# Unread bfloat16 products in TensorE's gaps, and projections that do not wait for their bias

## The chip, the cores and the metric

One core of a Trainium2 chip runs the whole program. The metric is the device time of one execution in microseconds. The engines are TensorE (PE, its weight loads PEld), VectorE (DVE), ScalarE (ACT), GpSimd (POOL) and SyncE (SP), which issues most transfers; ScalarE issues some too.

## The reference

A decoder layer over 32 sequences of 128 tokens with 128 features: causal self-attention (16 heads of 8), cross-attention to `ctx_1024`, and a mixture of 8 experts of which each token takes 2. Each of the three is followed by a sum with its input and a layer norm.

```python
x = _layernorm(x + _attn(x, x, x, sa_wq, sa_bq, ..., True), ln1_g, ln1_b)
x = _layernorm(x + _attn(x, encoder_output, encoder_output, ca_wq, ca_bq, ..., False), ln2_g, ln2_b)
x = _layernorm(x + _moe(x, router_w, router_b, e_w1, e_b1, e_w2, e_b2), ln3_g, ln3_b)
```

In `_attn`, `Q = q_in @ wq + bq` and `K = k_in @ wk + bk`; the scores are the softmax's argument. In `_moe`, the two experts with the largest router weights get `gelu(x w1 + b1) w2 + b2`. All is float32.

## The kernel before

The sequences are worked on in 8 groups of 4. For each group and each attention there is a chain: load `xin`, four transposes on TensorE into a PSUM bank, a copy to `xT` (ScalarE), the projections, then scores.

A projection of queries or keys is made by `parts`. One float32 product of 128x512 (`project`, line 841 in the profile) goes to a bank. ScalarE adds the bias column and rounds to bfloat16 (`p3[:, 0]`, line 916), VectorE takes the rest (`u`, line 920), GpSimd splits that into two further bfloat16 parts (lines 924 and 927; for the first group's queries it is VectorE). Then transfers (`qk<-p`, line 949) spread the parts over the rows of `qk`, so that one bfloat16 product of 64 rows yields a float32-like score. Scores are made twice: with queries on the partitions, for the maxima (VectorE, `nm`, line 1045), and with keys on the partitions, for the exponentials (ScalarE, `pr`, line 1513). The maxima are split, transposed (line 1066), copied (`nmT`) and sent by a transfer (`qk<-nmT`, line 1078) into spare rows of the queries; the second scores wait for that. After the last attention step come the experts' blocks (lines 1859 and 1876).

The order of work is not the order of the code. Each piece is a `Task` with an engine, a planned duration, a priority, what it depends on (`deps`) and the buffers it holds (`Buf`, whose places come from pools; `s_ps` is the PSUM pool `Banks`, four tiles `ps` of two halves). `Plan.run` simulates the engines with the planned durations: a free engine takes the ready task of lowest priority whose buffers can be had. The result, `plan.order`, is a list by planned start, and `Plan.emit` writes the instructions in that list's order. On the chip each engine then works through its own instructions strictly in that order, and waits on semaphores where data is not there. Planned times only set the order. `early` adds a task outside the attention chain, such as a memset; `t1` in `parts` is the product, `t2` ScalarE's part, and the last entry of the `deps` that `parts` is given is the load (or the computation) of the bias column.

Of the kernel before, what the change touches and what calls it, by code (L numbers as in the profile page):

```python
# [9 lines left out]
F32 = mybir.dt.float32  # L10
BF16 = mybir.dt.bfloat16
I32 = mybir.dt.int32
U32 = mybir.dt.uint32
AF = mybir.ActivationFunctionType
# [3 lines left out]
P = 128  # L18
# [17 lines left out]


AHEAD = 4.0
LINK = 0.07
LEAD = 0.4  # L40
SWITCH = 0.06
# [157 lines left out]
class Plan:  # L199
# [21 lines left out]
    def run(self):  # L221
# [17 lines left out]
        while left:  # L239
# [68 lines left out]
            if what is not None:  # L308
                t, kind = what
                if kind == "end":  # L310
# [4 lines left out]
                    for s in t.next:  # L315
                        s.n -= 1
                        if s.n == 0:
# [3 lines left out]
                            else:  # L321
                                k += 1
                                late = LEAD if s.lead and t.lead and t.lat < 1.0 else 0.0
                                heapq.heappush(events, (now + LINK + late, k, (s, "ready")))
                elif kind == "apart":
# [7 lines left out]
        self.order = order  # L333
        return max(t.end for _, _, t in order)

    def emit(self, tc):
        sync = mybir.DependencyInfo(mybir.DependencyClass.Sync, mybir.DependencyReason.DATA)
        seen = {}

        def line(i):  # L340
            return (i.engine, "DMA" in i.opcode)

        for _, _, t in self.order:
            bb = tc.nc.cur_bb.bb
            if t.rest:
                self.pause()
            n0 = len(bb.instructions)
            t.fn()
            t.ins = list(bb.instructions[n0:])
            if not t.own:  # L350
                continue
            need = dict.fromkeys(t.deps)
            for b in t.bufs:
                need.update(dict.fromkeys(b.before))
            kept = [i for u in need for i in u.ins]
            mine = t.ins[0]
            for u in need:
                for i in u.ins if any(line(j)[1] for j in u.ins) else u.ins[-1:]:
                    if line(i) != line(mine) or line(i)[1]:
                        tc.add_manual_dep(mine, i.name, sync, reason="data or place")  # L360
            for i in t.ins:
                for key, name in seen.items():
                    if key[0] != i.engine or (key[1] and line(i)[1] and t.eng == "POOL"):
                        tc.declare_no_dep(i, group=name, keep=kept, reason="apart, by the plan")
            for i in t.ins:
                name = seen.setdefault(line(i), f"{i.engine}{'q' if line(i)[1] else ''}")
                tc.add_to_no_dep_group(name, i)
# [3 lines left out]
def kernel(  # L371
# [34 lines left out]
    nc = tc.nc  # L406
# [12 lines left out]
    plan = Plan()  # L419
    add = plan.add  # L420

    def sb(shape, name, dtype=F32):
        return one.tile(shape, dtype, name=name)
# [5 lines left out]
    s_ps = Banks([psum.tile([P, 2, 512], F32, name=f"ps{i}") for i in range(4)], 2)  # L429
# [23 lines left out]
    def early(eng, dur, prio, fn, deps=()):  # L453
        return add(eng, dur, prio, fn, deps)
# [6 lines left out]
    def c_ident():  # L461
# [3 lines left out]
            fill=1.0, base=0, channel_multiplier=1,  # L465
        )

    t_ident = early("POOL", 0.7, -20, c_ident)
    t_ident16 = early("DVE", 0.3, -19.9, lambda: nc.vector.tensor_copy(ident16, ident), [t_ident])

# [157 lines left out]
    def pe(dur, prio, fn, deps, bufs, mode="128x128", lat=0.0):  # L628
        return add("PE", dur, prio, fn, deps, bufs, mode=mode, lat=lat)

    b_q = Buf(s_ps)
    t = pe(
        0.3, -4, lambda b=b_q: nc.tensor.matmul(b.at[:, 0:1], lhsT=wqcr, rhs=cols["b1"], start=True, stop=True),
        [t_wqcr, t_col["b1"]], [b_q],
    )
# [5 lines left out]
    for n, wo in (("s", "wos"), ("c", "woc")):  # L641
        bv = Buf(s_ps)
        t = pe(
            0.3, -9 if n == "s" else 3,
            lambda bv=bv, n=n, wo=wo: nc.tensor.matmul(
                bv.at[:, 0:P], lhsT=cols["bv" + n].broadcast_to([P, P]), rhs=raw[wo], start=True, stop=True
            ),
            [t_col["bv" + n], t_raw[wo]], [bv],
        )
# [14 lines left out]
    def c_rwg():  # L664
# [5 lines left out]
    t = pe(  # L670
        0.3, 3.6,
        lambda br=br: nc.tensor.matmul(
            br.at[:, 0:E], lhsT=cols["b2"].broadcast_to([P, P]), rhs=rw, start=True, stop=True
        ),
        [t_rw, t_col["b2"]], [br],
    )
# [13 lines left out]
    t = pe(0.2, 12, lambda bb=bb: nc.tensor.transpose(bb.at[:, 0 : E * NFC], b1r, ident[: E * NFC, : E * NFC]), [t_b1r, t_ident], [bb], "32x128")  # L690
# [128 lines left out]
    first = {}  # L819
# [19 lines left out]
    def project(bank, w, xT):  # L839

        nc.tensor.matmul(bank, lhsT=w, rhs=xT.rearrange("p s t -> p (s t)"), start=True, stop=True)  # L841
# [67 lines left out]
    def parts(w, b, xT, deps, prio, terms, name):  # L909


        bank, p3, r1, at = Buf(s_ps), Buf(s_p3), Buf(s_r1), Buf(s_q if name[0] == "q" else s_kk)
        t1 = pe(1.12, prio, lambda: project(bank.at, w, xT.at), deps, [bank, xT, p3])
        t2 = add(
            "ACT", act(512, 1), prio + 0.1,
            lambda: nc.scalar.activation(p3.at[:, 0, :], bank.at, AF.Identity, bias=b), [t1], [bank, p3],
        )
        t3 = add(
            "DVE", dve(512), prio + 0.2,
            lambda: nc.vector.scalar_tensor_tensor(r1.at, bank.at, b, p3.at[:, 0, :], ALU.add, ALU.subtract),  # L920
            [t2], [bank, p3, r1],
        )
        eng, ename, du = (nc.vector, "DVE", (0.32, 0.69)) if name == "qs0" else (nc.gpsimd, "POOL", (0.62, 1.16))
        t4 = add(ename, du[0], prio + -3.68, lambda: eng.tensor_copy(p3.at[:, 1, :], r1.at), [t3], [p3, r1])  # L924
        t5 = add(
            ename, du[1], prio + -2.28,
            lambda: eng.tensor_tensor(p3.at[:, 2, :], r1.at, p3.at[:, 1, :], ALU.subtract), [t4], [p3, r1],  # L927
        )
        soon = name in ("qs0", "ks0")
        again = name[0] == "q" and name not in ("qs0", "qs1")  # L930
        q, dq = ("ACT", nc.scalar) if name == "ks0" else ("SP", nc.sync)
        n = 1 if name[1:] == "s0" else 2 if name[1:] == "s1" else 3
        cleared = t_qz[0:n] if name[0] == "q" else t_qz[3 : 3 + n]
        t7 = []
        if again:
            t7.append(
                add(
                    q, 0.6, prio + 0.4,
                    lambda: dq.dma_start(out=at.at[3::4].rearrange("a i n -> a (i n)"), in_=zero_d), [t4, t_zero, *cleared],
                    [at], lat=3.0,  # L940
                )
            )
        for k, t_ in enumerate((t2, t4, t5)):
            for t in range(8):
                if terms[t] != k + 1:
                    continue

                def rows(t=t, k=k):
                    dq.dma_start(out=at.at[t::8], in_=p3.at[:, k, :])  # L949

                t7.append(
                    add(q, 0.6, (-23 + 0.1 * k if soon else prio + 0.37) + 0.01 * t, rows, [t_, *cleared], [p3, at], lat=2.6)
                )
                if soon:
                    it_store.setdefault(name, []).append(t7[-1])
        return at, t7, t5
# [510 lines left out]
    at = {}  # L1467
# [5 lines left out]
    for i in range(NT + NL):  # L1473
# [18 lines left out]
        for h in range(2):  # L1492
            if sk is not None:
                w = sk[2]
# [4 lines left out]
                else:  # L1499
                    nd = [itk.nmt["s", sk[1], "lo"], itk.nmt["s", sk[1], w]]  # L1500
                kp, tk = Buf(s_ps, 2), Buf(s_tk)
                t = pe(
                    time_k(sk), i + 0.5 * h - AHEAD, lambda sk=sk, h=h, kp=kp: scores_k(sk, h, kp.at),
                    [t_cols, *itk.t_Q, *itk.t_K, *nd], [kp, itk.Q, itk.K, itk.pr[w], tk],
                    "64x64" if sk[0] == "s" else "64x128",
                )
# [4 lines left out]
                te = add(  # L1511
                    "ACT", 1.02, i + 0.5 * h + 0.1 - AHEAD,
                    lambda kp=kp, prb=prb, h=h: nc.scalar.activation(  # L1513
# [8 lines left out]
            if sq is not None:  # L1522
                itq = items[sq[0], sq[1]]
                qp, tq = Buf(s_ps, 2), Buf(s_tq)
                t = pe(
                    time_q(sq), i + 0.5 * h + 0.49 - AHEAD, lambda sq=sq, h=h, qp=qp: scores_q(sq, h, qp.at),
                    [t_cols, *itq.t_Q, *itq.t_K, steps_k.get(i - LOCK)], [qp, itq.Q, itq.K, nm, tq],
                    "64x64" if sq[0] == "s" else "64x128",
                )
                step_tasks[i] = t  # L1530
                scores_all.append(t)
                ms.append(maximum(sq, h, qp, nm, i + 0.5 * h + 0.93 - AHEAD, t, tq))
        if sq is not None:
# [187 lines left out]
    def load_numbers(name, engine, tab, s, n):  # L1721
# [13 lines left out]
    t = pe(  # L1735
        0.12, X0 - 1.9,
        lambda: nc.tensor.matmul(bf.at[:, 0:E], lhsT=ones16, rhs=cg[:, NG - 1, :], start=True, stop=True),
        [cg_done[NG - 1]], [bf],
    )
# [13 lines left out]
    for e in range(E):  # L1753

        def fill(e=e):
            own = rows_d[P + e * REG : P + (e + 1) * REG, :]
            nc.sync.dma_start(out=own[bass.ds(t_places["all"][e], P), :], in_=fillrow)
# [212 lines left out]
    at = 0  # L1970
# [4 lines left out]
    s = 0  # L1975
    for gi in range(NG):
        done = 2 * G * (gi + 1) + E - 1
        s = max((done if gi >= GF else NF + max(E, done - NF)) - 1, s + 4 if gi else 0)
# [3 lines left out]
    idle = sb([P, 176], "idle")  # L1982
    plan.pause = lambda: nc.gpsimd.memset(idle, 0.0)
    plan.run()
    plan.emit(tc)


# [39 lines left out]
```

## Time and profile before

| | |
|---|---|
| median of 3 runs | 554.89 us (554.87 to 559.47) |
| profiled execution | 559.5 us, span 557.8 us |
| mean granted TensorE clock | 0.903 |
| PE busy | 449.5 us, 81% of the span |
| VectorE, ScalarE, GpSimd busy | 66%, 54%, 57% |
| share of the chain that ended last | PE 45%, DVE 17%, DMA 15%, POOL 7% |

The span goes from the first to the last instruction of one profiled execution, and the time of that execution is 1.7 us longer. The granted clock is a share of full speed. The chain that ended last is followed back from the last instruction, at each step to what released it. A product of two float32 tiles appears as two records.

### The profile page before, as it was taken

To read this page: it belongs to the slowest core of one execution; us is meant where nothing else is said; L and a number is where in the kernel's file an instruction comes from. 1 tells how busy PE (TensorE), PEld (TensorE's weight loads), DVE (VectorE), ACT (ScalarE), POOL (GpSimd) and SP (SyncE) were. 2 spreads that over 40 slices of the span, in tenths; PEclk is the share of its full clock that TensorE was granted. 3 is DMA by queue.
4 is the path that set the end of the run, shared out by engine and by line. 5 is a ranking of instruction groups with operands and counts; after the bars stand their busy time and mean duration, and the time that the engine had idled before them with its cause. 6 is when DMAs were issued, how large, how long until landed. Compare 5 with 4: busy or idle time off the path is not lost.

```text
span 557.8 us, 22749 instructions
## 1 busy us (share of the span) xinstructions
PE 449.5 (81%) x8571; PEld 355.3 (64%) x8571; DVE 368.3 (66%) x1063; ACT 303.1 (54%) x684; POOL 320.3 (57%) x589
## 2 busy tenths in 40 slices
PE   6648687788878979869798888758999989999930
PEld 3424564565555557557566566537899989999930
DVE  6477465587849748659566858884747412288887
ACT  3324345367355564645646745527676657778840
POOL 3742423433425774774773764834488888767771
PEclk9767898889979978898898989977999989999975
DMA  5776633756536466376353251267872988896432
GB/s 165 129 166 163 142 84 77 174 138 184 161 90 165 116 156 166 84 194 175 92 145 89 79 158 27 71 173 231 233 236 88 343 262 258 264 301 201 120 92 89
DMA packets 104748, 87.59 MB, mean 157 GB/s; under 512 B 24235, under 2 KB 91983, under 8 KB 104160
## 3 DMA queue, kind: packets, MB, share of 16 engines
q1 hardware_dynamic: 98736, 76.69, 50.6%
q0 software_dynamic: 4320, 8.47, 4.5%
q8 instruction: 69, 1.13, 0.9%
q10 hardware_dynamic: 1584, 0.98, 0.7%
q14 instruction: 39, 0.32, 0.2%
HBM read 43.23 MB, written 13.97 MB: 103 GB/s over the span
## 4 chain that ended last, share of the span: by engine, by line
PE 45%; DVE 17%; DMA 15%; POOL 7%; issue 6%; SPq 5%; ACT 3%; POOLq 0%; ACTq 0%; DVEq 0%
PE ps L985 12%; PE ps L1859 10%; PE ps L1876 10%; DMA qk<-p 8%; DVE nm L1045 6%; DMA qk<-nmT 3%; SPq L949 3%; PE ps L841 3%; ACT pr L1513 2%; PE ps L877 2%; POOL rows_d L1399 2%; POOL p L927 2%; PE ps L835 1%; PE ps L1290 1%; PE ps L1826 1%
## 5 line engine op out<-in xcount | busy, mean ns | idle before, releaser
L1045 DVE TENSOR_REDUCE nm<-ps 128x8 f32<-128x1024 f32 (+1 forms) x112 | 132.8, 1217 | 47.4 <-PE ps L985 46.2
L1513 ACT ACTIVATE pr<-ps 128x1024 f32<-128x1024 f32 x112 | 110.8, 1021 | 56.4 <-PE ps L985 52.9
L985 PE MATMUL ps<-qk,qk 64*128 64x128 bf16 (+2 forms) x3072 | 95.3, 226 | 39.8 <-DMA qk<-p 12.7
L985 PEld LDWEIGHTS <-qk 64*64 64x64 bf16 (+1 forms) x3072 | 65.5, 112 | 83.4 <-issue 31.4
L1399 POOL DMA_INDIRECT rows_d<-y,rid x64 | 64.9, 1014 | 35.9 <-issue 12.9
L985 PE MATMUL ps<-pr,v 64*32 64x128 f32 (+2 forms) x3072 | 74.4, 272 | 8.6 <-issue 7.0
L985 PEld LDWEIGHTS ps<-pr,v 64*32 64x32 f32 (+1 forms) x3072 | 59.1, 113 | 21.6 <-issue 14.3
L1859 PE MATMUL ps<-qk,qk 128*128 128x128 f32 x488 | 63.9, 279 | 0.0
L1859 PEld LDWEIGHTS ps<-qk,qk 128*128 128x128 f32 x488 | 59.6, 195 | 0.4 <-issue 0.4
L1908 POOL DMA_INDIRECT res_d<-p,id x49 | 48.2, 984 | 15.6 <-DVE st L1181 5.4
L1868 ACT ACTIVATE qk<-ps,b1c 128x128 f32<-128x128 f32 x160 | 45.2, 387 | 17.1 <-PE ps L1859 14.9
L1058 POOL CAST nmx<-nm 128x16 bf16<-128x16 f32 x64 | 13.0, 203 | 69.5 <-DVE nm L1045 67.3
L1876 PE MATMUL ps<-wall,qk 128*128 x320 | 42.1, 278 | 0.3 <-ACT qk L1835 0.3
L1868 ACT ACTIVATE k<-ps,b1c 128x128 f32<-128x128 f32 x124 | 35.1, 382 | 12.5 <-PE ps L1859 10.9
L1876 PEld LDWEIGHTS ps<-wall,qk 128*128 128x128 f32 x320 | 38.9, 194 | 0.6 <-ACT qk L1835 0.4
L1141 DVE STREAM_TRANSPOSE u<-ps 128x512 f32<-128x512 f32 x32 | 22.1, 702 | 25.9 <-PE ps L985 17.4
L927 POOL TENSOR_TENSOR p<-u,p 128x512 bf16<-128x512 f32 x31 | 35.8, 1157 | 1.6
L924 POOL CAST p<-u 128x512 bf16<-128x512 f32 x31 | 19.1, 615 | 25.8 <-DVE u L920 16.6
L1876 PE MATMUL ps<-wall,k 128*128 x248 | 32.2, 275 | 0.0
L1876 PEld LDWEIGHTS ps<-wall,k 128*128 128x128 f32 x248 | 29.8, 192 | 0.0
L1908 POOL DMA_INDIRECT res_d<-o,id x22 | 22.0, 998 | 12.6 <-DVE rti L1350 5.7
L1889 DVE TENSOR_SCALAR id<-xT,tab_e 128x1 int32<-128x1 f32 x47 | 12.2, 269 | 24.6 <-PE ps L1859 19.9
(295 smaller groups left out, 856.4 us busy)
## 6 DMA issues: line engine op xcount, KB each, us to landing
qk<-p SPq DMA_DIRECT2D x186, 128.0 KB
qk<-in_L_xattn_e_w_dram SPq DMA_DIRECT2D x61, 256.0 KB
qk<-zero_d SPq DMA_DIRECT2D x14, 256.0 KB
pr<-res_d SPq DMA_DIRECT2D x7, 512.0 KB
qk<-nmT SPq DMA_DIRECT2D x48, 64.0 KB
xT<-rows_d SPq DMA_DIRECT2D x47, 65.0 KB
w<-in_L_xattn_e_w_dram SPq DMA_DIRECT2D x10, 256.0 KB
xin<-in_x_dram SPq DMA_DIRECT2D x8, 256.0 KB
```

What stands on the lines that cost most here:

```text
L841: nc.tensor.matmul(bank, lhsT=w, rhs=xT.rearrange("p s t -> p (s t)"), start=True, stop=True)
L924: t4 = add(ename, du[0], prio + -3.68, lambda: eng.tensor_copy(p3.at[:, 1, :], r1.at), [t3], [p3, r1])
L927: lambda: eng.tensor_tensor(p3.at[:, 2, :], r1.at, p3.at[:, 1, :], ALU.subtract), [t4], [p3, r1],
L985: nc.tensor.matmul(out_, lhsT=lhsT, rhs=rhs, start=start, stop=stop, skip_group_check=True)
L1045: lambda: nc.vector.tensor_reduce(dst(), src(), AX.X, ALU.max, negate=True), [dep], [pair, nm, turn],
L1141: t = add("DVE", dve(512), prio, lambda: nc.vector.transpose(u1.at, bank.at), [dep], [bank, u1])
L1399: nc.gpsimd.indirect_dma_start(out=rows_d[:, :], out_offset=bass.IndirectOffsetOnAxis(ap=rid.at[:, i, k : k + 1], axis=0), in_=y.at[:, i, ...
L1513: lambda kp=kp, prb=prb, h=h: nc.scalar.activation(prb.at[:, 8 * h : 8 * h + 8, :].rearrange("p h q -> p (h q)"), kp.at.rearrange("p b n - ...
L1859: nc.tensor.matmul(p1.at[:, c * P : (c + 1) * P], lhsT=w1.at[:, c, :], rhs=x_()[:, i * P : (i + 1) * P], start=True, stop=True)
L1868: nc.scalar.activation(h.at[:, c, :], p1.at[:, c * P : (c + 1) * P], AF.Gelu, bias=b1c[:, bass.ds(numbers[s]["b1"] + c, 1)],)
L1876: nc.tensor.matmul(shared.at[:, i * P : (i + 1) * P], lhsT=h.at[:, c, :], rhs=flat[:, bass.ds(numbers[s]["w2"] + c * P, P)], start=c == 0, ...
L1908: nc.gpsimd.indirect_dma_start(out=res_d[:, :], out_offset=bass.IndirectOffsetOnAxis(ap=idb.at[:, 0:1], axis=0), in_=o.at, in_offset=None, ...
```

## The change

Two edits, and a third that serves the first.

After the plan has run, the new `Plan.fill` goes through TensorE's planned steps up to 45.0 us of planned time. Wherever the plan leaves at least 0.3 us between two steps, and a half bank of PSUM is unused over that gap, it puts in as many extra products as fit at 0.24 us each. Each multiplies the tile `warm` by itself (128x128 stationary, 128x512 moving, bfloat16) into that half bank, and nothing reads the result. They depend on `warm` being set and on the earlier uses of the half bank. `warm` is set to zero by a new memset on GpSimd, first of all its tasks. And the product in `parts` no longer depends on its bias column; ScalarE's first reading of the bank does instead.

```diff
+WARM = 0.24
+WARMED = 45.0
...
+    def fill(self, banks, product, first, upto):
...
+        steps = [t for _, _, t in self.order if t.eng == "PE" and t.began < upto]
+        made = []
+        at = first.end
+        for t in steps:
+            n = int((t.began - at) / WARM)
+            if t.began - at >= 0.3 and n:
...
+                if free:
+                    _, _, p, b = min(free, key=lambda f: f[:2])
+                    for i in range(n):
+                        d = Task("PE", WARM, lambda p=p: product(p.ap), [first, *(b.tasks if b else [])], [], 0.0, 0.0, "128x128", True)
+                        d.began, d.end = at + WARM * i, at + WARM * i + WARM
+                        made.append(d)
+            at = t.began + t.dur
+        self.order = sorted(self.order + [(d.began, 0, d) for d in made], key=lambda o: o[0])
...
+    warm = sb([P, 512], "warm", BF16)
+    t_warm = early("POOL", 0.3, -21, lambda: nc.gpsimd.memset(warm.bitcast(F32), 0.0))
...
-        t1 = pe(1.12, prio, lambda: project(bank.at, w, xT.at), deps, [bank, xT, p3])
+        t1 = pe(1.12, prio, lambda: project(bank.at, w, xT.at), deps[:-1], [bank, xT, p3])
         t2 = add(
             "ACT", act(512, 1), prio + 0.1,
-            lambda: nc.scalar.activation(p3.at[:, 0, :], bank.at, AF.Identity, bias=b), [t1], [bank, p3],
+            lambda: nc.scalar.activation(p3.at[:, 0, :], bank.at, AF.Identity, bias=b), [t1, deps[-1]], [bank, p3],
...
     plan.run()
+    plan.fill(
+        s_ps, lambda at: nc.tensor.matmul(at, lhsT=warm[:, 0:P], rhs=warm, start=True, stop=True), t_warm, WARMED
+    )
     plan.emit(tc)
```

43 unread products come of it, in six places of TensorE's list; otherwise every engine's instructions keep their order. After the edit the lines of the code stand 37 lower (line 841 is then 878), and 40 lower near the end.

TensorE's list begins with the transposes of the first group's input (`xin`) and the projections of its keys and queries (`wksp`, `wqsp`). Before:

```order
L2022 UNCONDITIONAL_BRANCH
L835 MATMUL ps_68<-ident,xin_134 128x128 x4
L835 MATMUL ps_68<-ident,xin_135 128x128 x4
L841 MATMUL ps_68<-xT_136,wksp 128x512
L841 MATMUL ps_68<-xT_136,wqsp 128x512
```

Of the change, where the first pair of rows stands 14 times:

```order
L2062 UNCONDITIONAL_BRANCH
L2023 LDWEIGHTS warm
L2023 MATMUL ps_65<-warm 128x512
...
L872 MATMUL ps_68<-ident,xin_135 128x128 x4
L872 MATMUL ps_68<-ident,xin_136 128x128 x4
L878 MATMUL ps_68<-xT_137,wksp 128x512
L878 MATMUL ps_68<-xT_137,wqsp 128x512
```

The 14 unread products stand ahead of all real work on TensorE.

The second place is the first group's second scores: after the transposed maxima of its last tile (`nmx_168`, 169 in the change) and a small product for the router's bias (`rw`), the next scores wait for the transfer of `nmT`. Before:

```order
L985 MATMUL ps_66<-maskk,id_73 64x4x64
L1066 LDWEIGHTS nmx_168
L1066 MATMUL ps_68<-ident_72,nmx_168 32x128
L672 MATMUL ps_67<-rw,col_b_104 128x8
L985 LDWEIGHTS qk_150
L985 MATMUL ps_65<-qk_147,qk_150 64x128
```

Of the change, where the pair of `warm` rows stands 20 times:

```order
L1022 MATMUL ps_66<-maskk,id_73 64x4x64
L1103 LDWEIGHTS nmx_169
L1103 MATMUL ps_68<-ident_72,nmx_169 32x128
L709 MATMUL ps_67<-rw,col_b_105 128x8
L2023 LDWEIGHTS warm
L2023 MATMUL ps_67<-warm 128x512
...
L1022 LDWEIGHTS qk_151
L1022 MATMUL ps_65<-qk_148,qk_151 64x128
```

The 20 stand between the router's small product and the scores that wait for `nmT`; two more stand some 40 rows before them, ahead of the two blocks of scores that end with the first row shown, and two some 80 rows after. The remaining five stand further up, four before and one after the values' projection of the third input.

More of the change, by code (lines that the diff above doesn't have):

```diff
@@ L334, in run @@
         return max(t.end for _, _, t in order)
+    def fill(self, banks, product, first, upto):
+        used = {}
+        for _, _, t in self.order:
+            for b in t.bufs:
+                if b.slots is banks:
+                    used.setdefault(b, []).append(t)
+        spans = {id(p): [] for hs in banks.halves for p in hs}
+        for b, ts in used.items():
+            for p in b.places:
+                spans[id(p)].append((min(t.began for t in ts), max(t.end for t in ts), b))
+        steps = [t for _, _, t in self.order if t.eng == "PE" and t.began < upto]
[4 more added lines that the diff above has]
+            if t.began - at >= 0.3 and n:
+                free = []
+                for hs in banks.halves:
+                    for p in hs:
+                        if all(e + 0.3 <= at or s >= t.began for s, e, _ in spans[id(p)]):
+                            past = [q for q in spans[id(p)] if q[1] <= at]
+                            q = max(past, key=lambda q: q[1]) if past else (0.0, 0.0, None)
+                            free.append((q[1], len(free), p, q[2]))
+                if free:
[6 more added lines that the diff above has]
+        self.order = sorted(self.order + [(d.began, 0, d) for d in made], key=lambda o: o[0])
     def emit(self, tc):
```

## The prediction

> **What bounds the kernel now.** I read the page's summary first, then the chain that ended last for the first 60 us, then the timeline and the busy times by stage there, since every unread product stands in that stretch.
>
> ```profile
> PE 449.5 (81%) x8571; PEld 355.3 (64%) x8571; DVE 368.3 (66%) x1063; ACT 303.1 (54%) x684; POOL 320.3 (57%) x589
> PEclk9767898889979978898898989977999989999975
> ```
>
> TensorE is the busiest engine (81%), and its granted clock dips in slices 2 to 4 of about 14 us each. That average hides the question; what counts is whether TensorE holds the chain in the first 50 us.
>
> ```profile
> 2.44 3.64 DMA col_bks<-in_L_xattn_sa_bk_dram
> 6.08 0.14 issue
> 6.22 3.27 PE ps L841 x4
> ...
> 9.52 0.70 ACT p L916
> 10.21 0.02 issue
> 10.23 0.65 SPq L949
> 10.88 0.05 issue
> 10.93 3.90 DMA qk<-p
> ...
> 14.90 5.01 DMA qk<-p
> ...
> 26.98 6.59 DMA qk<-p
> ...
> 40.42 2.32 DMA qk<-nmT
> 42.74 0.14 issue
> 42.88 0.88 PE ps L985 x16
> 43.75 0.02 issue
> 43.77 1.03 ACT pr L1513
> 44.81 0.04 issue
> 44.85 1.07 PE ps L985 x30
> 45.92 2.00 PE ps L841 x2
> 47.93 2.38 PE ps L985 x55
> ```
>
> TensorE holds it twice: from 6.22 to 9.49 (the first two projections) and from 42.88 to 50.31. Between 9.5 and 42.7 the links are SyncE's issues and the transfers `qk<-p` and `qk<-nmT`, which a faster product does not shorten. They pass on a delay of the first projections whole.
>
> **How fast products go at the two clocks.**
>
> ```profile
> 3.96 2.12 PE L835 MATMUL ps<-ident,xin 128*128 128x128 f32 x8 [3.96 <-DMA xin<-in_x_dram]
> 10.43 1.12 PE L841 MATMUL ps<-xT,wqsp 128*128 128x512 f32 x2
> 11.39 0.60 PE L835 MATMUL ps<-ident,xin 128*128 128x128 f32 x4
> 37.00 0.64 PE L985 MATMUL ps<-qk,qk 64*64 64x128 bf16 x16
> 37.65 0.64 PE L985 MATMUL ps<-qk,qk 64*64 64x128 bf16 x16
> 66.02 0.42 PE L985 MATMUL ps<-qk,qk 64*64 64x128 bf16 x16 [2.21 <-DMA qk<-nmT]
> 66.35 0.42 PE L985 MATMUL ps<-qk,qk 64*64 64x128 bf16 x16
> ```
>
> A block of scores has 16 products of 128 columns and 4 mask products of 256, on quarters of the array (64*64); I take four as running at a time: 4 x 128 + 256 = 768 columns in turn. From one block's start to the next's are 0.65 us at 37.00 and 0.33 us at 66.02, so a column costs 0.85 ns slow and 0.43 ns fast, and an unread product of 512 bfloat16 columns **0.43 us slow, 0.22 us fast**. A projection (two records) takes 1.12 us fast, half of 3.27 us when nearly all slow; four transposes 0.60 against half of 2.12.
>
> When the clock changes:
>
> ```profile
> 15.00:16.00 1.00, 0.00 (x0) 0.84 1.13 215
> 22.00:23.00 1.00, 0.66 (x24) 0.75 0.13 1
> 32.00:33.00 1.00, 0.00 (x0) 0.87 0.87 163
> 49.00:50.00 1.00, 1.00 (x68) 0.60 0.92 192
> 35.00:39.30 4.30, 4.21 (x45) 0.50 0.69 184
> 44.80:49.80 5.00, 4.95 (x128) 0.50 0.55 141
> L841 PE MATMUL ps<-xT,wqsp x16: 592/630/991, 8.1 to 241.5; 128*128 128x512 f32 x16
> ```
>
> In the first six rows the columns are stretch, length, TensorE's busy time with its count, granted clock, share and rate of the DMA engines. A mean of 0.84 between full and half speed puts the fall at 15.7, the others put a rise at 22.5, a fall at 32.7, a rise at 49.8. The rise at 49.8 came after 5.0 us of nearly unbroken work; 4.2 us from 35.0 lifted nothing. The clock column says 1.00 from the start, before any change is recorded, but the records don't agree: the first `wqsp` projection's record is the longest of 16 (991 ns, at 8.1), and the pair at 10.43 is fast. So the clock began slow and rose near 8.9, 4.9 us after work began at 3.96. I take **5 us of unbroken work** for a rise, with 4.2 and 6.4 us (the burst that began near 16.1 and was lifted at 22.5) as ends.
>
> [...]
>
> **The change part by part.** The 43 unread products stand in TensorE's list as 14, 4, 1, 2, 20 and 2; everything else keeps its order on every engine.
>
> *The bias wait.* The first projection began at 6.22; `col_bks` had landed at 6.08, and the eight transposes ended at 3.96 + 2.12 = 6.08 too. What goes is at most 0.14 us, and the transposes are late next. ScalarE's `p` takes the wait over; it comes after the product, two microseconds later. Value 0.
>
> *The memset on GpSimd.*
>
> ```profile
> 0.81 0.20 POOL L462 MEMSET ident<- 128x128 f32 x1 [0.29 <-POOLq L2009]
> 1.31 1.76 DVE L770 MEMSET qk<- 128x2048 f32 x1 [1.31 <-PEq L2009]
> 1.67 1.38 POOL L787 MEMSET v<- 128x1536 f32 x1
> ```
>
> 128x256 float32 lies between 0.20 and 1.38 us, nearest to the first: 0.3 us. The identity is then ready near 1.7, under the input's transfer that ends at 3.96. Cost 0, and 0.3 us for all of GpSimd's early work if that cover were gone.
>
> *The first 14.* They can begin when the memset is done and the engines are let go, about 1.3 (VectorE starts at 1.31). With a rise 5 us later, at 6.3, some 11.6 go slow (5.0 us) and 2.4 fast (0.5 us): they end at **6.9**, where the transposes began at 3.96. They stand ahead of the transposes in one queue, so the real work waits 2.9 us for nothing that it needs. Then it goes fast: first transposes to 7.5, second to 8.1, the copy beside them, projections from 8.2 at 1.12 each to 10.4. Before it was 9.49: **+0.9 us**. A rise after 4.2 us gives +0.4 (fill ends 6.4), after 6.4 us +1.5 (all 14 slow, to 7.3, transposes partly slow). Behind the projections are queued ScalarE's `p` and the transfers `qk<-p` of both queues, so this goes down the whole transfer chain.
>
> *The 4 and the 1.* Four go after 13.6, where TensorE waits until 16.1: 0.9 to 1.7 us in 2.5 idle. One goes before a projection that a transfer releases at 18.79. Cost 0. If they hold the clock up, the work at 16 to 21 us is faster, but it is not in the chain.
>
> *The 2, the 20 and the 2.*
>
> ```profile
> 35.03 2.04 PE L841 MATMUL ps<-xT,wksp 128*128 128x512 f32 x2 [3.47 <-DMA rw<-in_L_xattn_router_w_dram]
> 38.12 1.93 ACT L1513 ACTIVATE pr<-ps 128x1024 f32<-128x1024 f32 x2
> 38.64 0.60 PE L672 MATMUL ps<-rw,col_b 128*128 128x8 f32 x2
> 42.88 0.64 PE L985 MATMUL ps<-qk,qk 64*64 64x128 bf16 x16 [3.64 <-DMA qk<-nmT]
> 51.49 1.10 PE L841 MATMUL ps<-xT,wqsp 128*128 128x512 f32 x2 [0.64 <-issue]
> ```
>
> No unread product fills 28 to 35 us, so the clock has fallen when the projection of 35.03 begins, now 35.9. It takes 2.04 us, then two slow unread products 0.86, then scores to `L672`, which ends at 39.24 + 0.9 + 0.86 = 41.0. Work has been unbroken for 5 us: the rise is due here, and the 20 take 20 x 0.22 = 4.4 us, to **45.4**. The late scores also push `pr`, `nmT` and its transfer by 0.9 + 0.86, so without the 20 the next scores would begin at 44.6; with them at 45.4, **2.5 us after the 42.88 of before**. A rise 1.4 us later makes three of them slow: +0.6.
>
> From there the clock is up where it was half until 49.8. The stretch 42.88 to 50.31 loses: a block before the first `pr` 0.3; the block of 32 + 4 products (1024 columns) 0.4; the projection 2.00 - 1.10 = 0.9; the two blocks after it 0.8. That is 2.4, and leaves **+0.1** at 50.3. The last 2 go while TensorE waits for `pr` (0.44 in about 0.5): 0. But SyncE's queue and `nmT` were pushed by 1.8 us and gain nothing from the clock; the transfers of `p` behind them are late next. Between 0.1 and 1.8 I take the middle, **+1.0 us**.
>
> The sum is against the profiled execution: 559.5 us (span 557.8 and 1.7 around it), so 560.5. That execution lies 4.6 above the median of 554.89, on which the same +1.0 gives **555.9 us**.
>
> **The rivals.**
>
> *The warm clock is worth more (chance 0.25).* The clock stays up over 13.6 to 16.1, the first scores at 20.8 and VectorE's maxima come about 1.4 us earlier, and SyncE's delay is taken up in its own waits; the last term then is -2.4 from 42.88 on with only 0.9 + 0.4 given up, about -1.5: 553.4. Against it: the chain over 10 to 42 is transfers.
>
> *Nothing is left of it (0.20).* A shift at 50 us vanishes in later waits for transfers: 554.9, give or take 0.5.
>
> *The unread products don't lift the clock (0.10), the slower side.* Their operands are zeros, which no row of this trace shows. Then the first fill ends at 7.3 and what follows is as slow as before: 7.3 - 3.96 = +3.3. The 2 and the 20 are slow: 39.24 + 3.3 + 0.86 + 8.6 = 52.0 for the scores of 42.88, +9.1 and no gain after it: 564.0. It decides as soon as more than about half of the 20 go slow: then they outlast by over 2.4 us what the clock brings back. [...]
>
> **How the numbers follow.** My own case holds 0.45, from 554.5 (+0.4 at the head: the 20 end at 44.9, 2.0 late, and 2.4 comes back) to 557.3 (+1.5 at the head and 0.86 more on SyncE's queue, passed on whole). The first rival, with the same spread, begins at 552. Another execution of the kernel before took 559.47, so a median can fall 4.6 higher by the lot; the range takes most of that in: 551.5 to 560.5. The zeros case stays outside. A measurement tells about 1% from no change, 549.3 to 560.4: faster 0.04 (no case reaches it), same 0.84, slower 0.12 (the zeros, and a late rise in both places).
>
> **What would show it.** Right: 14 records of `ps<-warm` from 1.3 us, the first at some 0.43 us spacing, the last few at 0.22; transposes from about 6.9; the first `p` for queries near 10.4; granted clock 0.50 at 35 to 40, rising near 41; the 20 done about 45.4; the chain's time at `L985` after `nmT` later, its projection behind it near 1.1. Wrong: transposes at 4, unread products at 0.22 from the first, scores after `nmT` before 43, or a clock still half at 46.

## The result, and the profile after

| | before | changed |
|---|---|---|
| median of 22 executions each, same chip | 557.19 us | 560.28 us |
| lowest to highest | 549.15 to 564.07 us | 554.75 to 565.81 us |
| mean | 556.76 us | 560.24 us |
| profiled execution, span | 559.5, 557.8 us | 561.08, 559.3 us |

The change is slower by less than 1%: 3.5 us in the mean, with a standard error of 1.0 us. The ratio of the two is 1.0106, with a 95% interval of 1.0073 to 1.0139; it counts only executions within 1.5% of the fastest of their own kernel, which are 11 of 22 before and 19 of 22 after, so it lies above the ratio of all executions, 1.0063. That is why the experiments below give differences of means of all executions, each with its standard error.

The forecast was 555.9 us, +1.0 us on a base of 554.89. That base, a median of three, lay 2.3 us under the median of 22. So 4.4 us are to be explained: 2.3 of base, the rest of the change.

The summary and the clock of the page, changed kernel:

```profile
PE 455.1 (81%) x8610; PEld 355.4 (64%) x8614; DVE 368.3 (66%) x1063; ACT 303.3 (54%) x684; POOL 320.7 (57%) x590
PEclk9879799898979989899799979956999989999985
```

TensorE is 5.6 us busier. Slices 2 to 4 of the clock line read 8, 7 and 9 where 7, 6 and 7 stood, but slice 5 (56 to 70 us), which no unread product touches, reads 7 where 8 stood. The start, from TensorE's timeline of the changed kernel:

```profile
1.18 4.67 PE L2023 MATMUL ps<-warm 128*128 128x512 bf16 x14 [1.18 <-POOL warm L504]
5.68 1.04 PE L872 MATMUL ps<-ident,xin 128*128 128x128 f32 x8
6.95 1.12 PE L878 MATMUL ps<-xT,wksp 128*128 128x512 f32 x2 [0.24 <-ACT xT L898]
7.92 1.02 PE L878 MATMUL ps<-xT,wqsp 128*128 128x512 f32 x2
```

The 14 end at 5.85. The real work begins 1.7 us later than before but runs fast throughout: transposes 1.04 us where they took 2.12. ScalarE's timeline puts the first `p` for queries at 8.97, where it was 9.52:

```profile
8.97 0.69 ACT L953 ACTIVATE p<-ps,col_bqs 128x512 bf16<-128x512 f32 x1 [0.17 <-PE ps L878]
```

So in this one execution the head gained 0.55 us. The second place, same timeline of TensorE:

```profile
36.69 0.63 PE L2023 MATMUL ps<-warm 128*128 128x512 bf16 x1 [0.22 <-issue]
...
38.69 0.39 PE L709 MATMUL ps<-rw,col_b 128*128 128x8 f32 x2
38.93 4.48 PE L2023 MATMUL ps<-warm 128*128 128x512 bf16 x19
43.34 0.42 PE L1022 MATMUL ps<-qk,qk 64*64 64x128 bf16 x16
...
46.69 1.10 PE L878 MATMUL ps<-xT,wkcp 128*128 128x512 f32 x2 [1.03 <-DMA qk<-p]
...
51.80 0.28 PE L1022 MATMUL ps<-maskq,id 64*64 64x256 bf16 x4
54.01 1.10 PE L878 MATMUL ps<-xT,wksp 128*128 128x512 f32 x2 [1.93 <-POOL nmx L1096]
...
57.53 1.11 PE L872 MATMUL ps<-ident,xin 128*128 128x128 f32 x4 [0.34 <-ACT nmT L1110]
58.57 0.64 PE L1022 MATMUL ps<-qk,qk 64*64 64x64 bf16 x32
```

(Of the 2 and of the 20 the trace holds one record less.) The projection at `wkcp`, and the same steps at the end of that stretch, before:

```profile
45.85 2.07 PE L841 MATMUL ps<-xT,wkcp 128*128 128x512 f32 x2
...
52.76 0.28 PE L985 MATMUL ps<-maskq,id 64*64 64x256 bf16 x4
53.47 1.10 PE L841 MATMUL ps<-xT,wksp 128*128 128x512 f32 x2 [0.42 <-DMA qk<-p]
...
56.55 0.63 PE L835 MATMUL ps<-ident,xin 128*128 128x128 f32 x4 [0.39 <-ACT nmT L1073]
57.11 0.45 PE L985 MATMUL ps<-qk,qk 64*64 64x64 bf16 x32
```

The 20 take 4.48 us at full clock and the scores behind them start at 43.34, 0.46 us later than before. The projection of keys at `wkcp`, 2.07 us before, takes 1.10, but it waits 1.03 us for a transfer. Then TensorE waits 1.93 us ahead of the next projection of keys (0.42 before), and after that its work takes longer: transposes 1.11 where they took 0.63. The seventh `pr`, on ScalarE's timeline of the changed kernel:

```profile
63.76 1.94 ACT L1550 ACTIVATE pr<-ps 128x1024 f32<-128x1024 f32 x2 [2.76 <-PE ps L1022]
```

And before, 1.44 us earlier:

```profile
62.32 1.94 ACT L1513 ACTIVATE pr<-ps 128x1024 f32<-128x1024 f32 x2 [3.58 <-PE ps L985]
```

Why the wait: the row of the changed kernel names GpSimd's `nmx`, done at 53.94. But the semaphore events of the trace have the last of the transfers that this projection waits for landing at 53.88 (before: 53.33), so the transfers set the wait, but for 0.06 us. TensorE was done with the work ahead of it at 52.08, before at 53.04. Of the 1.5 us by which the wait grew, then, 1.0 is that TensorE came earlier, and 0.5 that the transfers landed later.

SyncE issues these transfers of `p` in its own queue, and it is late. Its timeline (start, length, line, transfer, count) in the changed kernel:

```profile
40.95 4.36 SPq L986 DMA_DIRECT2D qk<-p  x5
...
46.55 5.18 SPq L986 DMA_DIRECT2D qk<-p  x6
```

And before:

```profile
41.12 3.19 SPq L949 DMA_DIRECT2D qk<-p  x5
...
45.55 4.45 SPq L949 DMA_DIRECT2D qk<-p  x6
```

The six begin 1.0 us later and end 1.7 us later. The five ahead of them began earlier than before, but the last of the five, at 43.61, takes 1.70 us where it took 0.54. And why the slow stretch: in both traces all changes of the recorded clock (34 before, 30 in the changed kernel) are whole multiples of 3.41 us apart. So I read TensorE's busy time in the 3.41 us ahead of a change, from the busy times by stretch (columns: stretch, length, TensorE's busy time, weight loads, VectorE, ScalarE, GpSimd, granted clock, share and rate of the DMA engines). Changed kernel:

```profile
0.77:4.18 3.41, 3.00 (x8) 1.06 (x9) 2.75 (x9) 0.46 (x1) 2.62 (x9) 1.00 0.65 188
34.90:38.32 3.42, 3.20 (x41) 1.34 (x42) 1.76 (x4) 0.85 (x2) 1.14 (x4) 0.50 0.64 164
51.97:55.38 3.41, 1.48 (x26) 0.61 (x22) 1.97 (x4) 0.56 (x2) 1.52 (x4) 1.00 0.56 155
56.00:62.00 6.00, 5.31 (x135) 3.47 (x133) 4.98 (x6) 1.43 (x4) 2.25 (x5) 0.50 0.93 217
```

After the first two stretches (TensorE busy 88% and 94%) the clock rose, at 4.18 and 38.32. After the third, which holds the wait of 1.93 us and is 43% busy, it fell, at 55.38, and stayed half until 62.21. Before:

```profile
60.05:63.46 3.41, 1.74 (x104) 1.59 (x104) 0.96 (x2) 1.14 (x2) 2.56 (x6) 1.00 0.84 219
63.46:66.88 3.42, 1.21 (x64) 0.86 (x57) 0.19 (x1) 1.31 (x3) 0.00 (x0) 1.00 0.32 76
```

A stretch 51% busy kept the clock, the next, 35% busy, lost it at 66.88, behind the seventh `pr`. So in this pair the delay at the seventh `pr` comes with a sequence: TensorE early and transfers late, a wait on TensorE where there was nearly none, and the clock lost while TensorE is on the chain.

### The profile page after: what moved, and what is told of

Its sections match the earlier page's. It is cut to its first block, busy times and chain, and to the rows that moved or that the text cites. A ratio compares the mean times of both kernels' runs of the same rounds, so it can differ in the third digit from the quotient of the medians.

```text
span 559.3 us, 22831 instructions
## 1 busy us (share of the span) xinstructions
PE 455.1 (81%) x8610; PEld 355.4 (64%) x8614; DVE 368.3 (66%) x1063; ACT 303.3 (54%) x684; POOL 320.7 (57%) x590
## 4 chain that ended last, share of the span: by engine, by line
PE 46%; DVE 18%; DMA 11%; POOL 7%; issue 7%; SPq 5%; ACT 4%; DVEq 0%; POOLq 0%; ACTq 0%
PE ps L1022 14%; PE ps L1896 10%; PE ps L1913 10%; DVE nm L1082 7%; DMA qk<-p 6%; SPq L986 3%; ACT pr L1550 2%; PE ps L878 2%; PE ps L872 2%; DMA qk<-nmT 2%; POOL rows_d L1436 2%; PE ps L1327 1%; PE ps L1863 1%; POOL p L964 1%; SPq L596 1%
## 5 line engine op out<-in xcount | busy, mean ns | idle before, releaser
L1436 POOL DMA_INDIRECT rows_d<-y,rid x64 | 64.9, 1014 | 34.6 <-issue 13.4
L1022 PEld LDWEIGHTS ps<-pr,v 64*32 64x32 f32 (+1 forms) x3072 | 59.0, 113 | 19.4 <-issue 12.0
```

The lines of the kernel that those rows point to most:

```text
L1022: nc.tensor.matmul(out_, lhsT=lhsT, rhs=rhs, start=start, stop=stop, skip_group_check=True)
L1436: nc.gpsimd.indirect_dma_start(out=rows_d[:, :], out_offset=bass.IndirectOffsetOnAxis(ap=rid.at[:, i, k : k + 1], axis=0), in_=y.at[:, i, ...
```

## The experiments

Each difference is the mean of all executions less that of the kernel before in the same set of runs on the same chip, plus or minus its standard error, with the numbers of executions (this, before). The sets differ in level: the median of the kernel before was 557.19 and 561.21 us in two, and between 601.48 and 606.72 in four. "The stage" is the time from the third to the seventh `pr`, in the one profiled execution; "head" is the start of the first `p` for queries (before: stage 18.54, head 9.52).

**The parts apart, first round.** The bias edit alone, without unread products:

```diff
-        t1 = pe(1.12, prio, lambda: project(bank.at, w, xT.at), deps, [bank, xT, p3])
+        t1 = pe(1.12, prio, lambda: project(bank.at, w, xT.at), deps[:-1], [bank, xT, p3])
```

> Only the bias edit; no unread product, no memset. Each theory below gives no difference from the kernel before: within 1 us of its mean. What it shows beyond that is how far two like kernels stand apart when single executions spread over 15 us.

-0.7 ± 2.3 us (6, 11): nothing seen, with a wide error.

The changed kernel with the 14 alone, and with all but the 14:

```diff
-            if t.began - at >= 0.3 and n:
+            if t.began - at >= 0.3 and n and at == first.end:
```

> Of the 43 unread products only the first 14, with the bias edit. Head theory (in most executions the clock rises later than in the profiled one, the 14 end after 6 us, and the transfer chain passes the delay on): the mean is 2 to 3.5 us over the kernel before. Middle theory (the 20 ahead of the scores cost it): 0 to +0.5. Clock theory (what is lost or won comes from where the clock falls later in the program): 0, give or take 1.5, with a spread like before. In the profile the first p for queries should stand between 9.0 (rise at 4.2) and 11 us (rise at 7.6).

```diff
-            if t.began - at >= 0.3 and n:
+            if t.began - at >= 0.3 and n and at != first.end:
```

> The 29 other unread products, without the first 14, with the bias edit. Head theory: 0. Middle theory: +2 to +3.5, and in the profile the scores after nmT stand 1 us or more later than 42.9 plus what the head differs. Clock theory: 0, give or take 1.5.

The 14 alone: +1.3 ± 1.9 (6, 11), head 9.94, stage 18.15. The other 29: +3.8 ± 2.5 (6, 11), head 9.71, stage 19.40. So the 29 were suspected, but this round told little for sure. It also had fewer products by a larger planned time:

```diff
-WARM = 0.24
+WARM = 0.43
```

> The fill is made with 0.43 us for a product in place of 0.24: 8 at the head in place of 14, 11 in place of 20, 23 in all. At the head they end by 1.2 + 8 x 0.43 = 4.6 even when all go slow. Head theory: -0.5 to +0.5 against the kernel before, so 3 us better than the change. Middle theory: half of the change's loss is left, +1 to +1.7. Clock theory: 0, give or take 1.5.

23 products (8, 2, 1, 11 and 1): +0.2 ± 1.7 (5, 11; one execution is left out, see the end), head 7.74, stage 20.25.

**The clock near 55 us.** If the lost clock is the cost, unread products in the wait ahead of the late projection of keys should keep it up. Eight are put there:

```diff
+            if t is self.hold:
+                n, at = 8, t.began - 1e-4
...
+        if name == "ks3":
+            plan.hold = t1
```

> The change with 8 more unread products (1.8 us fast) right ahead of the projection that TensorE waited 1.6 to 2.1 us for near 54 us wherever the 20 stood. Gap theory (the 20 let TensorE finish early, the clock falls in the gap that this leaves, and the scores at 55 to 64 us go slow): the clock stays up past 62; from the first p for queries to the seventh pr are 53.5 us or less, where the change and the two other kernels with the 20 (or 11) had 54.8 to 55.0 and the kernels without 52.8 to 53.7; the mean time about 1.5 us under the change. Delay theory (the 20 push SyncE's queue and that stays): 54.8 or more, and the mean time is the change's.

+1.6 ± 0.9 (12, 29), and the change again, as it is:

> The change as it is, once more, for its own second profile and its times beside the other kernels on one chip. Head theory and gap theory together: 2 us over the kernel before in the mean (0.45 at the head, 1.6 by the gap); if the 3.5 us of the first comparison are all the change's, 3.5. First p for queries between 8.9 and 10.6 by when the clock rises, 54.5 to 55.5 us from there to the seventh pr, clock down for some time between 53 and 64.

+1.9 ± 0.8 (12, 29). The eight did stand in the wait (seven have a record), and the clock stayed up till 59.5 us, where I had expected past 62; but the stage was 20.2. TensorE's timeline with the eight:

```profile
52.28 1.67 PE L2029 MATMUL ps<-warm 128*128 128x512 bf16 x7 [0.16 <-issue]
53.79 1.02 PE L882 MATMUL ps<-xT,wksp 128*128 128x512 f32 x2
...
58.23 0.63 PE L876 MATMUL ps<-ident,xin 128*128 128x128 f32 x4 [1.82 <-DMA xin<-in_x_dram]
```

The next step then waited 1.82 us for its input. My theory that the half clock itself is the cost finds no support here: with the clock up, a transfer took its place, and in the time of the kernel no gain is seen (-0.3 ± 0.8 against the change again). It isn't excluded either, since the clock fell at 59.5, ahead of the seventh `pr` at 64.5. TensorE's wait at 54 us in the change again is put down to the transfer of `p`, and its clock falls at 54.81, after 48% busy:

```profile
55.36 2.05 PE L878 MATMUL ps<-xT,wksp 128*128 128x512 f32 x2 [2.10 <-DMA qk<-p]
```

The busy times ahead of the fall in the same kernel:

```profile
51.40:54.81 3.41, 1.65 (x26) 0.61 (x22) 3.27 (x5) 0.90 (x2) 1.00 (x5) 1.00 0.85 153
```

The two comparisons of the change give together **+2.5 ± 0.6 us**.

**Without the 20.**

```diff
-            if t.began - at >= 0.3 and n:
+            if t.began - at >= 0.3 and n and (n < 15):
```

> The change without the 20. Gap theory and delay theory alike: no wait of over 1 us ahead of that projection, clock up at 54 to 62, and 52.8 to 53.7 us from the first p to the seventh pr. If 54.8 or more stay, the 20 are not the cause and the 4, 1, 2 or 2 are. Mean time 1.6 us under the change.

+5.2 ± 1.7 (4, 29), stage 20.92. The loss doesn't need the 20. TensorE's timeline has the wait here too:

```profile
54.91 1.10 PE L878 MATMUL ps<-xT,wksp 128*128 128x512 f32 x2 [2.02 <-DMA qk<-p]
```

**The head's size.** Eight products at the head alone (planned at 0.43 us), and the same again in another set:

```diff
-WARM = 0.24
+WARM = 0.43
...
-            if t.began - at >= 0.3 and n:
+            if t.began - at >= 0.3 and n and at == first.end:
```

> Only a fill at the head, sized with 0.43 us for a product: 8 products, no others. They end by 4.6 us; the clock rises between 4.2 and 7.6, so the first p for queries stands at 7.7 to 8.9 us, where the kernel before had 8.5 to 9.5. If a gain at the head passes down the transfer chain, the mean is 1 us under the kernel before, and 52.8 to 53.7 us follow to the seventh pr. If it is taken up on the way, 0.

> The kernel with 8 products at the head alone, once more. Head theory: 1 us under the kernel before, the first p at 7.7 to 8.9. First comparison: 1.1 under, with a standard error of 1.3.

-1.1 ± 1.3 (10, 29) and -0.5 ± 1.4 (12, 23), together -0.8 ± 1.0; heads 8.70 and 8.50. Six, with `n = min(n, 6)`:

> Only 6 products at the head, which end by 1.2 + 6 x 0.43 = 3.8, before the first input has landed near 4.0. Transposes at 4.0 to 4.2, clock up between 4.2 and 7.6, first p for queries at 7.4 to 8.8; 0.5 to 1.5 us under the kernel before, fast class. If such a gain is taken up on the way: 0.

+0.9 ± 1.6 (12, 35), head 10.02: the clock rose only at 10.1 there, where I had expected 7.6 at the latest (4.18 and one spacing of 3.41). And 42 in place of 14, all else of the change in place:

```diff
+                more = 3 if at == first.end else 1
...
-                    for i in range(n):
+                    for i in range(n * more):
```

> The change with 42 unread products at the head in place of 14. The 28 more go fast, 28 x 0.22 = 6.2 us: the first p for queries near 16. If a delay at the head is passed down the transfer chain one for one (the prediction's step, and the head theory), the mean is 6.2 us over the change, some 8 over the kernel before. If the chain takes part of it up later, less; then the 14 can't be what costs the change its 2 us.

+7.5 ± 1.5 (12, 23), 5.0 ± 1.6 more than the change. TensorE's timeline:

```profile
1.17 12.06 PE L2024 MATMUL ps<-warm 128*128 128x512 bf16 x42 [1.17 <-POOL warm L505]
13.07 1.04 PE L873 MATMUL ps<-ident,xin 128*128 128x128 f32 x8
```

ScalarE's timeline of the same kernel:

```profile
16.37 0.69 ACT L954 ACTIVATE p<-ps,col_bqs 128x512 bf16<-128x512 f32 x1 [0.17 <-PE ps L879]
```

The head is 6.8 us later than the mean of six profiles with 14 there (9.6). Against the change's own profile it is 7.4 us later, and so is the seventh `pr` (71.11 against 63.76): up to there a delay of the head is passed on whole, as the prediction read the transfer chain. At the end 5.0 ± 1.6 us are left, which agrees with that but can't show it.

**The middle's size.** 60 in place of 20, with `more = 3 if n > 14 else 1`:

> The change with 60 in place of the 20. The 40 more cost 40 x 0.22 = 8.8 us ahead of the scores that wait for nmT. The prediction's step says they pass whole, less what the clock brings back: 7 to 9 us over the change. If transfers bound the stage behind it and TensorE has time there, 4 to 7, and then the change's 20, which outlast the transfer by 1 us or less, cost next to nothing.

+8.2 ± 1.8 (6, 23). TensorE's timeline:

```profile
40.15 13.11 PE L2024 MATMUL ps<-warm 128*128 128x512 bf16 x60
53.19 0.42 PE L1023 MATMUL ps<-qk,qk 64*64 64x128 bf16 x16
```

The seventh `pr`, from ScalarE's timeline of the same kernel:

```profile
68.05 1.94 ACT L1551 ACTIVATE pr<-ps 128x1024 f32<-128x1024 f32 x2 [1.62 <-DVE nm L1083]
```

The scores are 9.9 us later than in the change, the seventh `pr` 4.3, the end 5.7 ± 1.9. So in this pair of profiles over half of a delay in the middle is taken up before the seventh `pr`: there it is not one for one. At the end the two ways can't be told apart.

**The 29 again, and their groups apart.** The 29 in another set:

> The 29 without the first 14, once more, since the first comparison had a standard error of 2.5 us. If the 14 carry the change's 2 us, 0 to +0.5 here; if the rest carries them, +1.5 to +2.

+4.5 ± 1.3 (6, 23), stage 21.39; with the first time +4.4 ± 1.1. Then each group alone, by the condition on `n`: `n > 14` (the 20), `n == 2` (the two pairs), `n in (1, 4)`:

> Only the 20. In all seven profiles so far that held any of the 2, 20 and 2, the clock fell again between 53 and 66 us and 19.4 to 21.4 us lay between the third and the seventh pr; in the five without them 17.7 to 18.8. Early rise theory (unread products near 40 us raise the clock before TensorE is on the chain; it then waits for transfers, the clock falls, and the next dense stretch goes slow): slow class here, and 1.4 us or more over the kernel before. If the 20 are harmless: fast class, 0.

> Only the two pairs of 2, ahead of the second scores' first blocks and behind them. The first pair goes slow and pushes pr by 0.9 us. Early rise theory: the pair closes a gap, so the clock may rise near 39 as in the kernel without the 20; slow class and 1 us or more over the kernel before. If only the 20 count: fast class, 0 to 0.9.

> Only the 4 and the 1 at 13 to 18 us, where TensorE waits anyway. Every theory: 0, fast class. If it is 1.5 us or more over the kernel before, these cost what the kernel without the 20 lost.

The 20 alone +1.4 ± 1.1, stage 16.42; the pairs alone -2.0 ± 1.2, stage 18.36; the 4 and the 1 alone 0.0 ± 1.1, stage 17.60 (12, 35 each). I had expected one group to carry the cost; none is away from nothing by twice its error. The 20 alone can't be told from nothing, nor from the whole change's +2.5.

**Two groups together, and the pairs again.**

```diff
-            if t.began - at >= 0.3 and n:
+            if t.began - at >= 0.3 and (n == 2 or n > 14):
```

> The change with only the 2, the 20 and the 2 (24 products), without the 14, the 4 and the 1. Theory that the products around 35 to 45 us cost as a group (clock raised near 40, down again near 55, TensorE waiting about 2 us for a transfer ahead of the projection of keys near 54): 19.4 us or more from the third to the seventh pr, and +2 to +4.5 us in the mean over the kernel before. Rival, that the cost needs the 4 and the 1 as well: below 18.8 us, clock up past 60, and the mean within 1 us of the kernel before.

> The change with only the two pairs of unread products, as once before (-2.0 +/- 1.2 us in the mean, not told from nothing). If that was real, -1 to -3 us again; if it was the lot of the runs, within 1 us of the kernel before. The stage from the third to the seventh pr stays near 18 us either way.

The 20 and the pairs: +2.2 ± 1.1 (12, 23), stage 19.19, a little under the 19.4 expected. The pairs again: -0.2 ± 1.0 (12, 23), both times together -0.9 ± 0.8, so the gain of the first time was not confirmed; and the stage was 19.63, where I had expected 18. TensorE's timeline of the kernel with the 20 and the pairs:

```profile
53.75 1.10 PE L878 MATMUL ps<-xT,wksp 128*128 128x512 f32 x2 [2.22 <-DMA qk<-p]
...
58.72 0.63 PE L872 MATMUL ps<-ident,xin 128*128 128x128 f32 x4 [2.26 <-DMA xin<-in_x_dram]
```

The same of the pairs alone, second time:

```profile
51.79 1.13 PE L878 MATMUL ps<-xT,wksp 128*128 128x512 f32 x2
...
57.64 0.63 PE L872 MATMUL ps<-ident,xin 128*128 128x128 f32 x4 [3.08 <-DMA xin<-in_x_dram]
```

The wait of 2.22 us for the transfer of `p` is back with the two groups, and gone with the pairs alone.

**All together.** A split that I chose after seeing the runs: kernels with at least two of the three groups behind the head (the change twice, the 29 twice, the smaller sizes, without the 20, the 20 with the pairs) have +2.8 ± 0.4 us, weighted by their errors; those with at most one of them (the bias edit, the heads of 14, 8, 8 and 6, each group alone, the pairs twice) -0.1 ± 0.4. The three kernels with still more products are left out. Kernels of one set share their comparison, so these errors are a little small; one fit to all executions of these kernels, with a level for each set, gives +3.0 ± 0.5 and -0.1 ± 0.5. In the profiles the first seven wait 1.6 to 2.2 us ahead of the projection of keys near 54 us, and their stages take 19.2 to 21.4 us; the other ten, the kernel before among them, wait 0 to 1.0 us there, and their stages take 16.4 to 19.6. SyncE begins the six transfers of `p` at 46.75 in the mean of the first seven, at 45.55 in that of the others. In six of the seven, one of the three issues just ahead of the six takes 1.4 to 2.1 us; otherwise these take 0.4 to 0.7, but for one of 1.2 us in the other ten. Nothing in the traces tells what stretches that one issue.

ScalarE's instructions come in one order in all seventeen, so their profiles can be laid side by side. Here each difference is the mean of the seven less that of the ten. The first `p` for queries stands alike (-0.1 ± 0.4 us). At the sixth `pr` the seven are 1.1 ± 0.4 us ahead: so much the clock has brought. From there to the seventh `pr` they take 13.7 to 15.2 us and the ten 10.7 to 13.4, with no overlap, and at the seventh the seven are 1.8 ± 0.5 us behind. On the way, TensorE is ready for the late projection 1.1 us earlier and begins it 0.7 us later; the transposes behind it begin 1.6 us later. The lag is 2.7 ± 0.6 us at the 19th `pr` (117 us) and 2.8 ± 0.9 at the 41st (173 us); further on the profiles spread too far. So the loss arises ahead of 117 us, most of it between the sixth and the seventh `pr`. (The sets' different levels have no part in that: up to 256 us they are some 1 us apart at most, and nearly all of their 45 us come behind 360 us.)

No version beat the kernel before by more than twice its error.

## Why the prediction was wrong, point by point

- **Bias wait (0):** nothing seen, -0.7 ± 2.3. **Memset (0):** the 14 began at 1.18 behind it, and the transposes were not held by the identity. Both stand, the first within a wide error.
- **First 14 (+0.9 at the head):** the mechanism was right, the size too large. They took 0.43 us each, then 0.22; the clock rose at 4.2 us here (taken: 6.3), at 6.2 with the 14 alone, and at 7.0 in the change again, with heads at 8.97, 9.94 and 10.37 (forecast 10.4). The mean of six profiled heads with the 14 is 9.6, that of nine without unread products there 9.2: +0.4, and the 14 alone give +1.3 ± 1.9 at the end. What I treated as one rise, 5 us after work begins, came 3.0, 5.0 and 5.8 us after the first of the 14 in these three profiles, the first and the last of them of the same kernel.
- **The 4 and the 1 (0):** alone 0.0 ± 1.1. Whether they cost beside the other groups isn't settled: no run had them with the pairs or the 20 only, and with the 14 and the pairs (the kernel without the 20) there were +5.2 ± 1.7.
- **The 2, the 20 and the 2 (+0.1 at 50 us, SyncE +1.0):** this is the step that failed. The clock rose at 38.3 and the 20 ran fast, as said. The scores began at 43.34, not 45.4, since the 20 began at 38.93, not 41.0; 1.4 us of that is the head, which was that much earlier than forecast in this execution. SyncE's delay came out at 1.0 us in the pair of profiles and 1.2 in the groups, as forecast. What failed is what the last term, +1.0 us, is made of. It has TensorE level with before at 50.3 us and takes the late transfers to cost their own delay and nothing more. Instead the warm clock brought TensorE ahead: the sixth `pr` began at 49.40, before at 50.37 (1.1 ± 0.4 us earlier in the groups), although TensorE had waited 1.03 us for a transfer at `wkcp`. That lead was no gain, since the transfers were no faster (from the last of SyncE's six issues to the last landing that `wksp` waits for 3.9 us in both profiles: 50.03 to 53.88, before 49.39 to 53.33). TensorE waited 1.93 us at `wksp`, where it had waited 0.42, and the clock fell at 55.4 and was half up to 62.2, where it had been up before. At the seventh `pr` the change was 1.4 us late (1.8 ± 0.5 in the groups), and 2.7 ± 0.6 at the 19th. The prediction has no wait of TensorE behind 50.3 us and no fall of the clock there. The whole forecast, +1.0 us, measured +2.5 ± 0.6.
- **The rivals:** the clock rose at 4.18 over unread products of zeros alone, so the rival of the zeros falls. That the warm clock is worth more falls too: nothing is faster than before by more than twice its error. (Its sum was wrong as well: -2.4 with 0.9 and 0.4 given up is -1.1, not -1.5.) That nothing is left falls with +2.5 ± 0.6. I had no rival in which waits made by the change cost the clock later.
- **The base:** the +1.0 was put on 554.89. The kernel's executions spread over 15 us, and three of them gave a base 2.3 us too low. With +2.5 ± 0.6 for the change, this is half of what the forecast missed. The measured 560.28 lies just inside the range, whose upper end of 560.5 had been set for a slow lot of executions. So the range held by the room left for the base, not by a right account of the change.

**What stays open:** which property of the 29 goes with the stretched issue in SyncE's queue, when each group alone costs nothing that can be told; the sum of the single parts (the 14, the 4 and 1, the pairs, the 20), +1.7 ± 2.5, doesn't contradict the whole, so small costs that add up are not excluded. How much of the lag at the seventh `pr` is the clock's is open too. The one try to keep it up did not bring the time back, so the clock's fall is shown to follow the wait, but not to be the cost. Over the whole execution the granted clock is no lower with the change: 0.908 in the mean of the 12 executions of the change again, 0.904 in the 29 of the kernel before beside them. Single profiles mislead here: in the first pair the change is even with the kernel before again later (aligned starts 0.4 us earlier at 97 and 0.6 at 305 us), and the 1.6 us between their ends arise where the clock was half for longer (from 362 to 383 us the granted clock is 0.51 against 0.76, and TensorE does 193 products against 205).

## What to carry to other kernels

In the changed kernel the clock rose at 38.3 us, where it had risen at 49.8, and TensorE was ready 1.0 us earlier for a projection that waits for transfers. The gain turned into a wait (1.93 us where there had been 0.42), and the clock fell at 55.4, behind a stretch 43% busy. Before filling gaps, find the queue that feeds the engine and ask whether the fill delays it. And where executions spread by 15 us, take a base from some twenty of them before a change of 0.5% is forecast or judged.

## What the runs showed of the hardware

- The clock rose over unread products of zeros alone: in the changed kernel 3.0 us after the first of them (1.18 to 4.18), with no other work on TensorE.
- The clock fell after stretches that were far from idle. I cut each trace into stretches of 3.41 us, counted back from each change, and took the union of the matmul records in each: in the trace of before, the 17 that ended in a fall were at most 57% busy, and of 112 that kept the clock all but two were at least 59%; in the changed kernel 15 (at most 57%) and 117 (at least 58%). That is no threshold: the two others in the trace of before, 46% and 51% busy, kept the clock, and stretches of 55% to 57% lost it. Rises behind the first came after stretches at least 97% busy before (16) and 89% in the change (14); but in the trace of before one stretch that was busy throughout, from 107.83 us, did not lift the clock.
- The phase of those stretches was not the same in two executions of one kernel: the first rise fell at 4.2 us in one profile of the changed kernel and at 7.0 in the other, and the 14 took 4.67 and 6.07 us. Over the profiled kernels it lay anywhere from 4.2 to 10.5 us (10.5 with the 20 alone).
- One execution of the smaller sizes took 1313.44 us, with a recorded clock of 1.0; nothing in the runs explains it.
